# A GRU with a residual on one core: one block of GpSimd sums a step earlier, step 118 divided otherwise, nine units in front of the first state product

## The chip, the core and the metric

The kernel runs on one core of a Trainium2 chip. The metric is the device time of one execution in microseconds (us). TensorE (PE in the profile) multiplies matrices and writes into PSUM, VectorE (DVE) and ScalarE (ACT) read PSUM and SBUF, GpSimd (POOL) does elementwise work on SBUF, SyncE (SP) issues DMAs.

## The reference

x has 64 sequences of 128 steps with 512 features; h0 is 64 x 512. The output is x plus the states of a gated recurrent unit:

```python
z = sigmoid(concat([x_t, h]) @ Wz + bz)
r = sigmoid(concat([x_t, h]) @ Wr + br)
h_cand = tanh(concat([x_t, r * h]) @ Wh + bh)
h_new = (1.0 - z) * h + z * h_cand
h_next = where(prop, tanh(h_new @ Wp + bp), h_new)   # prop: every fourth step, not the last
# out[:, t] = x[:, t] + h_new
```

The products of h depend on the step before and must run one step behind the other; those of x do not.

## The kernel before

**The state products.** The batch of 64 is cut into two halves of 32, which are two Python generators, `half(0)` and `half(1)` (line 836). A loop at the end (line 947) runs whichever has issued less so far, so their instructions alternate in PE's queue. Each step does, per half: the R gate (`gate(R, ...)`, four products of h with 128 rows each), sigmoid on ACT, r*h and its turn (`rhT`, a transpose) on DVE; the Z gate; the H gate, which needs `rhT`; tanh on ACT; then on DVE the new h in three operations (L912, L921, the turn L251 into `hT`). In every fourth step the product with Wp follows. These products are the lines "rec<-wh" and "rec_z<-wh" of the profile.

**The x products as filler.** While PE would wait for ACT and DVE, it runs units of the x products from one list, `queue`. `fill(n, h)` (line 416) issues the next n units of a half. How many stand at which place of a step is written out by hand in `PLACES`, `HEAD` (line 626) and `TAIL` (line 627): three numbers per step, for the units behind the Z gate (line 903), behind the H gate (line 930) and behind the product with Wp (line 942). A step without an entry of its own uses `PLACES` by its place u in a period of eight; u = 3 has (6, 8, 0) and so has u = 2. Step 118 is `T - 10`, step 117 is u = 2. Before step 0, `both(n)` (line 632) runs the first n units for both halves, and step 0 has a fill of its own between the R and Z gates (line 863).

**The fast product.** For steps 2 and 3 the units are plain (`plain`, line 459): one unit is one block of 128 features and one gate. From group 1 (steps 4 to 7) on, the x products of groups of four steps are formed by a scheme of Strassen's kind on two levels: 7 outer blocks, each by 7 inner products, with sums of weights and of x formed beforehand and sums of results afterwards. `sum_inner(i)` (line 312) makes the sums of weights of outer block i: four operations, L318 to L321, of 128x384 elements. `sum_raw12`, `sum_raw4` and others make sums of x, each by `four` (line 325; L329 to L332), into buffers such as `s12r` and `s4r` that exist once. `batch` (line 483) makes the units of two blocks: 14 units, in an order fixed by their PSUM banks a, x or y, q and r. At certain units an `end` function runs behind the second half's unit: ACT copies a bank (L514), DVE adds it into `mb` (L531, L532, L537, L540, L541). `end_r2` (line 539; L540 and L541) is the last of a batch; L540 is the last reader of bank scratch_r, which the next batch writes again. The results are then summed on GpSimd (`pair_left`, `pair_right`, the `outer_` functions; L575 and L580 in the profile) into `cp`, and ACT seeds the gates' PSUM with that (L398).

**GpSimd's order.** Its instructions run in the order in which the generators write them. `behind_r` (line 724) is called by the second half behind the R gate, `behind_step` (line 757) at the end of a step. Around the change the order is: step 1 makes the sums of block 6, step 2 `pair_left(0, 1, 2)` in `behind_r`, then `sum_raw12(2)`, `sum_s12(2)` and the output's add (L811); step 3 `pair_right(0, 1, 10)` and `sum_inner(7)` in `behind_r`, then `pair_left(1, 8, 9)`, `pair_right(1, 8, 11)`, `sum_s34(2)`; step 4 `sum_inner(4)`; steps 5 and 6 the first sums of group 2, with `sum_raw4(2)` into `s4r`.

Of the kernel before, what the change touches and what calls it, by code (L numbers as in the profile page):

```python
# [18 lines left out]
def kernel(  # L19
# [14 lines left out]
    nc = tc.nc  # L34
    B, T, D = x.shape
# [7 lines left out]
    K = D // P  # L43
# [187 lines left out]
    def gate(i, h, lT, w):  # L231
        for k in range(K):
            products(gate_ps(i, h), h, lT[:, h, ts(k, V)], lambda c: quarters(w)[:, c, k])
            yield S * J
# [47 lines left out]
    def inner(i, ka, na):  # L282
        return OPERAND[i](ka)[:, :, :, ts(na, J // 4)]

    def leftover(i):
        return din[:, i - 1] if i <= 3 else inner(i, 0, 1)
# [25 lines left out]
    def sum_inner(i, eng, gates=slice(0, 3)):  # L312
        def of(v):
            return v[:, :, gates]

        t = [of(tt[:, i - 1, n]) for n in range(3)]
        v = {ab: of(inner(i, *ab)) for ab in ((0, 0), (0, 1), (1, 0), (1, 1))}
        eng.tensor_sub(t[1], v[1, 1], v[0, 1])  # L318
        eng.tensor_add(t[0], t[1], v[0, 0])
        eng.tensor_sub(t[2], v[1, 0], t[0])  # L320
        eng.tensor_sub(of(leftover(i)), v[0, 1], v[0, 0])  # L321
# [88 lines left out]
    def put(units):  # L410
        for unit, cols, bank, end, read in units:
            queue.append((unit, cols, reader.get(bank, -1), end))
            for b in read:
                reader[b] = len(queue) - 1

    def fill(n, h):
        for _ in range(n):
            if place[h] == len(queue):
                return
            unit, cols, after, end = queue[place[h]]  # L420
            while h == 0 and after >= place[1]:
                yield 0
            unit(h)
            yield cols
            place[h] += 1
            if h == 1 and end is not None:
                end()
# [31 lines left out]
    def plain(t, gates=(R, Z, H_)):  # L459
        order = [(e, k) for e in gates for k in range(K)]  # L460
        if t == Q4 - 1:
            order = [(e, k) for k in range(K) for e in gates]
        return [
            plain_unit(
                t,
                e,
                k,
                k == 0,
                *((lambda: add_bias(t, gates), gates) if t > 1 and (e, k) == order[-1] else ()),
            )  # L470
            for e, k in order
        ]
# [101 lines left out]
    def add(dst, a, b):  # L574
        nc.gpsimd.tensor_add(dst, a, b)  # L575

    def with_bias(g, i, v):
        m = M[g, i].rearrange("p b d g u -> p b (d g u)")
        v = v.rearrange("p d g u -> p (d g u)")
        nc.gpsimd.tensor_add(m, m, v.unsqueeze(1).to_broadcast([P, 2, 3 * J]))  # L580

    def c_block(g, a, nb):
        new_cp(2 * g + a)
        return flat(cp[2 * g + a][:, nb])

    def m_(g, i):
        return flat(M[g, i])
# [17 lines left out]
    def outer_u2(g):  # L605
        add(m_(g, 7), m_(g, 7), m_(g, 6))
# [7 lines left out]
    def pair_left(a, p1, p2, g=1):  # L614
        with_bias(g, p2, bias0)
        add(c_block(g, a, 0), m_(g, p1), m_(g, p2))

    def pair_right(a, p1, x_, g=1):
        with_bias(g, x_, bias_x[:, 1])
        add(c_block(g, a, 1), m_(g, p1), m_(g, x_))  # L620
# [4 lines left out]
    )  # L625
    HEAD = {0: (4, 6, 0), 1: (8, 6, 0), 2: (16, 12, 0), 3: (8, 6, 8), 4: (6, 8, 0)}
    TAIL = {
        T - 10: (5, 9, 0), T - 9: (1, 7, 5), T - 8: (1, 7, 0), T - 7: (1, 5, 0), T - 6: (0, 5, 0),
        T - 5: (0, 4, 3), T - 4: (0, 5, 0), T - 3: (0, 4, 0), T - 2: (0, 4, 0), T - 1: (0, 0, 0),
    }  # L630

    def both(n):
        for _ in range(n):
            for h in range(S):
                for _ in fill(1, h):
                    pass
# [42 lines left out]
    sum_outer(3)  # L679
    later_loads()  # L680
    put(plain(2, (R, Z)) + plain(3) + plain(2, (H_,)))
    both(6)

    state = {0: (h_init, hT)}

# [38 lines left out]
    def behind_r(t, duo, u):  # L724
        odd = FIRST + 2 * duo + 1
        if t == 2:
            pair_left(0, 1, 2)
        elif t == 3:
            pair_right(0, 1, 10)
            sum_inner(7, nc.gpsimd)  # L730
        if t == 4:
            sum_inner(4, nc.gpsimd)
        if u == 0 and duo >= 1 and odd - 2 < LAST:
            outer_u2(odd - 2)
# [101 lines left out]
    def half(h):  # L836

        for t in range(T):
# [10 lines left out]
            if h == 1:  # L849
                behind_r(t, duo, u)  # L850
# [9 lines left out]
                join(t, duo, u, 0)  # L860

            if t == 0:
                yield from fill(2 * K, h)
            yield from gate(Z, h, hT, wh[Z])
            keep = new_two("keep", t)
            z_ = z
# [79 lines left out]

    LAG = 700
    halves = [half(0), half(1)]
    at = [0, LAG]
    live = [True, True]  # L950
    while any(live):
        h = 0 if live[0] and (not live[1] or at[0] <= at[1]) else 1
# [46 lines left out]
```

## Time and profile before

| | us |
|---|---|
| median of 3 runs | 1262.54 (1262.44 to 1262.56) |
| the profiled execution | 1262.99 |
| its span, first to last instruction | 1261.0 |
| TensorE busy in it | 1250.6 |
| GpSimd busy in it | 891.3 |
| granted TensorE clock, mean | 0.999 |

A row of a timeline is: start and length in us, engine, line of the kernel, operation, what it writes and what it reads, partitions by elements, count; in brackets the idle time of the engine before it and what ended that. The rows of PE merge matmuls of one kind. A product of one unit is several records, and the two halves work side by side on different columns of the array.

### The profile page before, as it was taken

What the parts mean: (1) busy time and instruction counts of PE and PEld (TensorE: products, weight loads), DVE (VectorE), ACT (ScalarE), POOL (GpSimd) and SP (SyncE); (2) the same over time, 40 slices, a digit from 0 to 9 for tenths busy, and PEclk for the clock granted to TensorE, in tenths of its full rate; (3) what the DMA queues carried; (4) which work ended last, traced back from release to release, by engine and by line L of the source; (5) the groups of instructions that cost most, each with busy time, mean ns of one, the idle gap of its engine ahead of it and who ended that gap; (6) DMA issues with size and microseconds to landing.
All of it is one profiled execution on the core that took longest, in us unless ns stands there. A gap on an engine that the chain in (4) does not pass through costs nothing.

```text
span 1261.0 us, 60731 instructions
## 1 busy us (share of the span) xinstructions
PE 1250.6 (99%) x25960; PEld 1157.8 (92%) x25960; DVE 804.7 (64%) x2171; ACT 835.6 (66%) x2685; POOL 891.3 (71%) x1033
## 2 busy tenths in 40 slices
PE   9999999999999999999999999999999999999998
PEld 4898899999999999999999999999999999999875
DVE  4665666666666666666666666666666666666544
ACT  2566666666666766666676667666676766667665
POOL 3898867777776778767778677777777687677530
PEclk9999999999999999999999999999999999999999
DMA  8311111111121111221211111111111111111010
GB/s 238 92 27 44 46 45 51 38 50 40 37 53 44 45 45 28 53 53 37 53 28 44 53 43 47 39 47 40 53 36 53 40 33 53 48 42 36 7 43 24
DMA packets 113172, 60.82 MB, mean 48 GB/s; under 512 B 12776, under 2 KB 109288, under 8 KB 112904
## 3 DMA queue, kind: packets, MB, share of 16 engines
q1 hardware_dynamic: 111172, 54.97, 16.4%
q8 instruction: 205, 3.36, 1.1%
q10 hardware_dynamic: 1476, 1.84, 0.5%
q14 instruction: 63, 0.52, 0.1%
q0 software_dynamic: 256, 0.14, 0.1%
HBM read 40.11 MB, written 16.78 MB: 45 GB/s over the span
## 4 chain that ended last, share of the span: by engine, by line
PE 94%; POOL 2%; DMA 1%; SPq 1%; DVE 0%; issue 0%; ACT 0%; ACTq 0%; POOLq 0%; DVEq 0%
PE rec L222 43%; PE rec_z L222 16%; PE scratch_r L222 13%; PE scratch_q L222 10%; PE scratch_a L222 5%; PE scratch_x L222 4%; PE scratch_y L222 4%; POOL cp L575 1%; SPq L821 1%; POOL mb L580 1%; DMA wx<-in_L_cond_Wz_dram 1%; DMA xr<-in_x_dram 0%; DMA out_dram<-xr 0%; POOL xr L811 0%; POOL mb L575 0%
## 5 line engine op out<-in xcount | busy, mean ns | idle before, releaser
L222 PE MATMUL rec<-wh,rhT 128*32 128x256 f32 x4096 | 376.2, 379 | 0.0
L222 PE MATMUL rec<-wh,hT 128*32 128x256 f32 x3072 | 282.6, 379 | 0.4 <-DVE hT L251 0.4
L222 PE MATMUL rec_z<-wh,hT 128*32 128x256 f32 x3072 | 282.6, 379 | 0.0
L222 PEld LDWEIGHTS rec<-wh,rhT 128*32 128x32 f32 x4096 | 248.8, 110 | 20.1 <-ACT rec L398 0.9
L248 ACT ACTIVATE scratch_r<-rec 64x128 f32<-64x128 f32 x512 | 128.0, 250 | 137.7 <-PE rec L222 69.5
L398 ACT COPY rec<-cp 64x256 f32<-64x256 f32 x512 | 189.8, 371 | 20.6 <-DMA xr<-in_x_dram 1.1
L222 PEld LDWEIGHTS rec_z<-wh,hT 128*32 128x32 f32 x3072 | 192.2, 110 | 9.3
L222 PEld LDWEIGHTS rec<-wh,hT 128*32 128x32 f32 x3072 | 186.2, 110 | 14.6 <-ACT z L248 1.2
L248 ACT ACTIVATE rec_z<-rec_z 64x128 f32<-64x128 f32 x488 | 122.0, 250 | 91.8 <-PE rec_z L222 80.3
L248 ACT ACTIVATE c<-rec 64x128 f32<-64x128 f32 x512 | 138.9, 271 | 61.7 <-PE rec L222 50.1
L811 POOL TENSOR_TENSOR xr<-xr,h 128x256 f32<-128x256 f32 x127 | 93.0, 732 | 92.0 <-DVE h L921 89.3
L575 POOL TENSOR_TENSOR mb<-mb,mb 128x768 f32<-128x768 f32 x58 | 106.2, 1831 | 67.0 <-DVE mb L541 67.0
L575 POOL TENSOR_TENSOR cp<-mb,mb 128x768 f32<-128x768 f32 x76 | 139.0, 1829 | 8.1 <-DVE mb L541 4.4
L575 POOL TENSOR_TENSOR cp<-mb 128x768 f32<-128x768 f32 x46 | 84.2, 1831 | 56.8 <-ACT rec_z L398 55.4
L222 PE MATMUL scratch_r<-tw,s 128*32 128x192 f32 x928 | 120.8, 326 | 0.0
L514 ACT COPY cq<-scratch_q 128x384 f32<-128x384 f32 x212 | 102.1, 481 | 19.8 <-PE scratch_q L222 18.4
L531 DVE TENSOR_TENSOR cx<-scratch_r,cx 128x384 f32<-128x384 f32 x106 | 59.0, 557 | 84.8 <-PE scratch_r L222 67.5
L222 PE MATMUL scratch_q<-tt,s 128*32 128x192 f32 x928 | 103.6, 326 | 0.0
L873 DVE SCALAR_TENSOR_TENSOR keep<-rec_z,h 128x256 f32<-128x256 f32 x91 | 38.6, 424 | 95.8 <-ACT rec_z L248 88.5
L537 DVE TENSOR_TENSOR mb<-scratch_q,cx 128x384 f32<-128x384 f32 x106 | 59.1, 557 | 62.5 <-ACT cq L514 62.5
L853 DVE TENSOR_TENSOR rh<-scratch_r,h 128x128 f32<-128x128 f32 x192 | 56.0, 292 | 61.6 <-ACT scratch_r L248 61.6
L222 PE MATMUL rec<-wp,hT 128*32 128x256 f32 x992 | 91.5, 379 | 0.1
(188 smaller groups left out, 3840.0 us busy)
## 6 DMA issues: line engine op xcount, KB each, us to landing
out_dram<-xr SPq DMA_DIRECT2D x249, 64.0 KB, 1.8
xr<-in_x_dram SPq DMA_DIRECT2D x248, 64.0 KB, 2.0
xs<-in_x_dram SPq DMA_DIRECT2D x240, 64.0 KB, 2.0
wx<-in_L_cond_Wr_dram SPq DMA_DIRECT2D x2, 512.0 KB, 4.9
wx<-in_L_cond_Wz_dram SPq DMA_DIRECT2D x1, 1024.0 KB, 7.0
wx<-in_L_cond_Wh_dram SPq DMA_DIRECT2D x1, 1024.0 KB, 10.0
wp<-in_L_cond_Wp_dram SPq DMA_DIRECT2D x4, 256.0 KB, 5.7
wh<-in_L_cond_Wr_dram ACTq DMA_DIRECT2D x2, 256.0 KB, 4.7
```

Source lines behind the costliest of these rows:

```text
L222: nc.tensor.matmul(ps[part(2 * h + c)], lhsT=left, rhs=rhs(c), start=start, stop=True, skip_group_check=True,)
L248: nc.scalar.activation(dst[ts(d, 2 * V)], gate_ps(i, h)[ts(h, 2 * V), d, :], func)
L398: nc.scalar.copy(gate_ps(i, h)[rows].rearrange("p d (c n) -> p d c n", c=C), G[t][rows, :, :, i, :].rearrange("p c d n -> p d c n"),)
L514: nc.scalar.copy(c[:, :nm], ps[:, :nm])
L531: nc.vector.tensor_add(T2[what][:, :nm], r_ps[:, :nm], T2[what][:, :nm])
L537: nc.vector.tensor_add(blocks(1, 1), runs(q_ps[:, :nm]), runs(T2[what][:, :nm]))
L575: nc.gpsimd.tensor_add(dst, a, b)
L580: nc.gpsimd.tensor_add(m, m, v.unsqueeze(1).to_broadcast([P, 2, 3 * J]))
L811: nc.gpsimd.tensor_add(xr[g][:, j], xr[g][:, j], h_new)
L821: nc.sync.dma_start(out=out[ts(h, V), t - n + 1 : t + 1, ts(q, J)], in_=xr[g][part(q), j - n + 1 : j + 1, h, :],)
L853: nc.vector.tensor_mul(rh[:, h, :], r_, h_old[:, h, :])
L873: nc.vector.scalar_tensor_tensor(out=keep[:, part, :], in0=z_[:, part, :], scalar=1.0, in1=h_old[:, part, :], op0=ALU.subtract, op1=ALU.mult,)
```

## The change

Three places are edited. The four sums of the seventh inner block are written in step 2 instead of step 3. In step 118 six units of x stand behind the Z gate and eight behind the H gate, instead of five and nine. Nine units instead of six are issued in front of the first state product, and step 0's own fill has 5 units instead of 8 (K is 4). The instructions are the same in number and kind.

```diff
     TAIL = {
-        T - 10: (5, 9, 0), T - 9: (1, 7, 5), T - 8: (1, 7, 0), T - 7: (1, 5, 0), T - 6: (0, 5, 0),
+        T - 10: (6, 8, 0), T - 9: (1, 7, 5), T - 8: (1, 7, 0), T - 7: (1, 5, 0), T - 6: (0, 5, 0),
...
     put(plain(2, (R, Z)) + plain(3) + plain(2, (H_,)))
-    both(6)
+    both(9)
...
         if t == 2:
             pair_left(0, 1, 2)
+            sum_inner(7, nc.gpsimd)
         elif t == 3:
             pair_right(0, 1, 10)
-            sum_inner(7, nc.gpsimd)
...
             if t == 0:
-                yield from fill(2 * K, h)
+                yield from fill(2 * K - 3, h)
             yield from gate(Z, h, hT, wh[Z])
```

## The prediction

> **What bounds the kernel now.** The page comes first: its span and the busy time of each engine.
>
> ```profile
> span 1261.0 us, 60731 instructions
> PE 1250.6 (99%) x25960; PEld 1157.8 (92%) x25960; DVE 804.7 (64%) x2171; ACT 835.6 (66%) x2685; POOL 891.3 (71%) x1033
> ```
>
> TensorE (PE) computes for 1250.6 of 1261.0 us; no other engine passes 71%. No edit takes a matmul away, so the change can win only from the 10.4 us in which PE stands still, or lose by making PE stand still elsewhere. Second view: what PE waited for (total, times, longest).
>
> ```profile
> PE scratch_x L222 <- POOL s4r L331: 1.1, 1, 1.1
> PE scratch_r L222 <- DVE mb L540: 0.8, 1, 0.8
> ```
>
> The two longest each happen once, so each has a place; the others lie at the start, where the first loads are awaited, or are 0.2 us. The table by stretches finds it (length, then busy time of PE, PEld, DVE, ACT, POOL; clock, DMA).
>
> ```profile
> 20.00:25.00 5.00, 5.00 (x95) 3.03 (x91) 3.95 (x10) 0.20 (x1) 0.83 (x2) 1.00 1.05 254
> 100.00:105.00 5.00, 3.89 (x87) 3.32 (x82) 3.14 (x9) 2.45 (x8) 4.92 (x7) 1.00 0.14 37
> 1180.00:1190.00 10.00, 9.19 (x198) 7.62 (x191) 5.75 (x18) 6.13 (x21) 6.16 (x4) 1.00 0.01 2
> ```
>
> PE loses 1.11 us between 100 and 105 us, where GpSimd (POOL) is busy throughout, and 0.81 us between 1180 and 1190. From 20 to 25 us, where the third edit works, it loses nothing. The clock is 1.00 in all three.
>
> **First edit: the seventh inner block's sums.** Busy time counts the modelled tail of the matmul before a wait, so I price a stop by starts. The timeline of PE around it:
>
> ```profile
> 100.79 0.36 PE L222 MATMUL scratch_a<-wx,xT 128*32 128x192 f32 x2
> 100.83 0.39 PE L222 MATMUL rec<-wh,rhT 128*32 128x256 f32 x2
> 100.95 0.36 PE L222 MATMUL scratch_a<-wx,xT 128*32 128x192 f32 x2
> 102.42 0.36 PE L222 MATMUL scratch_x<-tt,s4r 128*32 128x192 f32 x2 [1.11 <-POOL s4r L331]
> 102.44 0.41 PE L222 MATMUL rec<-wh,rhT 128*32 128x256 f32 x2
> ```
>
> One half of the batch starts a pair every 0.16 us (100.79, 100.95); its next comes at 102.42: 1.47 - 0.16 = 1.31 us lost. The other half, which needs nothing from POOL, loses as much, since PE keeps its order: 102.44 - 100.83 = 1.61, less the 0.22 us at which its pairs of 256 columns follow each other (48 records, four at a time, in 2.59 us, in the rows of the third edit), 1.39. Mean 1.35 us. Now the POOL timeline that leads there:
>
> ```profile
> 54.24 1.83 POOL L575 TENSOR_TENSOR cp<-mb 128x768 f32<-128x768 f32 x1
> 60.49 0.46 POOL L329 TENSOR_TENSOR s12r<-xT 128x128 f32<-128x128 f32 x1 [4.42 <-PE scratch_r L222]
> 68.30 1.84 POOL L575 TENSOR_TENSOR cp<-mb,mb 128x768 f32<-128x768 f32 x1
> 70.09 1.01 POOL L318 TENSOR_TENSOR tt<-tw 128x384 f32<-128x384 f32 x1
> 74.20 1.85 POOL L580 TENSOR_TENSOR mb<-mb,bias_x 128x768 f32<-128x768 f32 x1
> 102.05 0.32 POOL L331 TENSOR_TENSOR s4r<-xT 128x64 f32<-128x64 f32 x1
> ```
>
> POOL idles 4.42 us before 60.49: the buffer s12r is free only when PE has read it. The four sums of block 7 run from 70.09 to 74.20. By starts they take 74.20 - 70.09 = 4.11 us. In step 2 they stand behind pair_left, whose last add (54.24) ends at 56.07, so they run until 56.03 + 4.11 = 60.14, 0.35 us before the next sum starts anyway. Their input tw[3] is POOL's own, written earlier in its queue, and nothing reads their results before the batches of group 2. Cost there: 0, covered by the idle time. The Trainium skill (Perfetto Trace Analysis, GPSIMD Engine Instruction) calls POOL's spans unreliable and starts the better clock; four spans of 1.01 as in the L318 row would give 4.04 and a spare of 0.42, and the same answer.
>
> What it frees is not 4.11 us. The instruction behind, pair_left for blocks 8 and 9, adds a bias to sums that DVE writes last here:
>
> ```profile
> 72.02 0.55 DVE L541 TENSOR_TENSOR mb<-scratch_x,cq 128x384 f32<-128x384 f32 x1
> 91.16 0.55 DVE L541 TENSOR_TENSOR mb<-scratch_x,cq 128x384 f32<-128x384 f32 x1
> 95.89 1.83 POOL L575 TENSOR_TENSOR mb<-mb,mb 128x768 f32<-128x768 f32 x1
> ```
>
> They are complete at 72.57, so POOL now waits from 70.1 to about 72.6 and starts 74.20 - 72.6 = 1.6 us earlier than before. From there to 102 it has no idle time, and I went through its inputs: the tightest is a block that DVE ends at 91.71 and POOL takes at 95.89, then at 94.3, still 2.6 us later. So the third sum of s4r ends at 102.37 - 1.6 = 100.8. PE wants it at 100.95 + 0.16 = 101.11, its weight load at 100.95. The wait goes, with 0.15 to 0.3 us to spare. **Worth 1.35 us**; bounds 0 (POOL held again) and 1.39. Behind 102 us both PE (1.35) and POOL (1.6) are earlier, so POOL's lead grows; the stores of step 3 and the loads behind them on SP's queue leave 1.6 us earlier, needed by nobody then.
>
> **Second edit: step 118.** The stop in PE's timeline, then DVE's timeline of step 118 and of step 117, which already runs with six and eight units:
>
> ```profile
> 1180.01 0.36 PE L222 MATMUL scratch_q<-wx,xT 128*32 128x192 f32 x2
> 1180.06 0.33 PE L222 MATMUL scratch_x<-tt,s4r 128*32 128x192 f32 x2
> 1181.20 0.36 PE L222 MATMUL scratch_r<-tw,s4r 128*32 128x192 f32 x2 [0.81 <-DVE mb L540]
> 1181.21 0.36 PE L222 MATMUL scratch_x<-tt,s12r 128*32 128x192 f32 x2
> ```
>
> ```profile
> 1167.98 0.56 DVE L537 TENSOR_TENSOR mb<-scratch_q,cx 128x384 f32<-128x384 f32 x1 [0.37 <-ACT cq L514]
> 1168.46 0.55 DVE L540 TENSOR_TENSOR mb<-scratch_r,cq 128x384 f32<-128x384 f32 x1
> 1177.82 0.56 DVE L537 TENSOR_TENSOR mb<-scratch_q,cx 128x384 f32<-128x384 f32 x1 [0.47 <-ACT cq L514]
> 1180.39 0.31 DVE L251 STREAM_TRANSPOSE hT<-h 128x128 f32<-128x128 f32 x1
> 1180.63 0.52 DVE L540 TENSOR_TENSOR mb<-scratch_r,cq 128x384 f32<-128x384 f32 x1
> ```
>
> Lost: 1181.20 - 1180.01 - 0.16 = 1.03 and 1181.21 - 1180.06 - 0.16 = 0.99, mean 1.01 us. Cause: with five units behind the Z gate, the batch's last unit comes behind the H gate, so DVE gets the read of its bank (L540) behind both turns of h (1180.39), and the next batch's first unit on scratch_r waits for it. In step 117 the sixth unit lies ahead of the H gate and L540 follows L537 at once; L537 of the two steps lies 9.84 us apart, so L540 will start near 1168.46 + 9.84 = 1178.30 and end at 1178.9, over 1 us before PE asks. Queued behind L540 and L541 on DVE are the state's own three operations, as in step 117, behind which the next state product starts at 1171.10:
>
> ```profile
> 1171.10 0.41 PE L222 MATMUL rec<-wh,hT 128*32 128x256 f32 x2
> ```
>
> No wait stands before it. Both steps do 14 units, so what follows keeps its place. **Worth 1.01 us**; bounds 0 and 1.03.
>
> **Third edit: nine units first.** Three units go from between the R and Z gates of step 0 to ahead of the R gate.
>
> ```profile
> 20.21 2.77 PE L222 MATMUL scratch_q<-wx,xT 128*32 128x256 f32 x48
> 22.80 1.50 PE L222 MATMUL rec<-wh,hT_init 128*32 128x256 f32 x20
> 21.66 0.65 DVE L264 STREAM_TRANSPOSE xT<-xr 128x256 f32<-128x256 f32 x1
> 27.05 0.31 DVE L251 STREAM_TRANSPOSE rhT<-rh 128x128 f32<-128x128 f32 x1
> 31.43 0.39 PE L222 MATMUL rec<-wh,rhT 128*32 128x256 f32 x2
> ```
>
> Six units take 22.80 - 20.21 = 2.59 us, so three take 1.30 and the R gate starts at 24.10. The ninth unit is the first on x of step 3; it starts at 20.21 + 8 x 0.43 = 23.67, and its transpose ends at 22.31: 1.36 us in hand. The last rhT moves from 27.36 to 28.66; the H gate keeps its place at 31.43, so the cover shrinks from 4.07 to 2.77 us and still holds. PE has no idle time to win here. **0**; bounds 0 and the 0.22 us of one pair.
>
> **The sum.** 1.35 + 1.01 + 0 = 2.36 us. The profiled execution took 1262.99 us (span 1261.0 and 2.0 outside it), 0.45 above the median of the runs, 1262.54. I carry the difference over: 1260.6 for a profile, **1260.2 us** for the runs. 0.2% of 1262.54, about what a measurement of this kernel can tell from no change, is 2.5 us: the forecast falls just inside.
>
> **The rivals.**
> *POOL is held again.* If anything between 72.6 and 100.8 holds POOL for d us, all but the spare 0.3 comes back as waiting for s4r. For it: the spare is small, and 4.92 of 5 us busy leaves no slack to catch up in. Against: every input that I followed is there. With half of the 1.35 gone: 1260.9; with all, 1261.5.
> *Step 118 only moves its wait.* L540 and L541 (0.9 us of DVE) now stand ahead of the state's operations; if step 119's first product then waited for hT, most of 1.01 would return: 1261.1. Against: step 117's rows.
> *Slower than before: the sums miss the gap.* If they can start only at 60.4, with the instruction that now ends the idle time, the chain behind shifts by 4.11 us. It leads to ACT and PE in step 3:
>
> ```profile
> 70.17 0.38 ACT L398 COPY rec_z<-cp 128x256 f32<-128x256 f32 x1 [0.43 <-POOL cp L575]
> 71.08 0.56 DVE L537 TENSOR_TENSOR mb<-scratch_q,cx 128x384 f32<-128x384 f32 x1 [0.75 <-ACT cq L514]
> 72.52 0.34 PE L222 MATMUL scratch_q<-wx,xT 128*32 128x192 f32 x2
> ```
>
> ACT already waits for POOL's add (68.30) there; behind that copy in its queue stands the one that DVE's L537 needs, and L537 is the last reader of scratch_q. It ends at 71.64, 0.88 us before PE writes the bank at 72.52. A shift of 4.11 stops PE for 3.2 us; the s4r wait then vanishes by itself (-1.35), step 118 gives -1.01: 1263.4. Shifts beyond 0.9 cost time; the kernel gets slower from 3.2. Against: all inputs of the sums stand earlier in POOL's own queue.
> *The sums fit, but run longer beside DVE.* The row of that stretch:
>
> ```profile
> 55.00:60.00 5.00, 5.00 (x122) 4.51 (x118) 2.80 (x8) 2.52 (x8) 1.07 (x1) 1.00 0.40 96
> ```
>
> If POOL stood still whenever DVE works, the sums would take up to 2.8 us longer, pass the gap by 2.45 and stop PE for 1.6: 1261.8. Against: between 70.09 and 74.20 three adds of DVE (71.08 to 72.57) run beside the same sums, and 4.11 contains that. The Trainium skill (SBUF — State Buffer, Who interferes with whom) has a DVE operation with two SBUF inputs and a reading GpSimd one lock each other out; DVE's adds here take one input from PSUM (rec_z, scratch), which by that section never locks.
>
> **How the numbers follow.** Forecast 0.69 (1259.8 to 1260.6, from the bounds, the pair and a tenth for the reading of starts); POOL held 0.15; step 118 0.08; slower 0.04; longer beside DVE 0.02; others 0.02. The range reaches to POOL's full loss and leaves the last three out: 1259.8 to 1261.5. Faster by over 0.2% means below 1260.0: a third of the forecast's case, 0.23. Slower by over 0.2% (above 1265.1) needs a shift of POOL by 5.8 us, or a cause that I don't see: 0.03. Same: 0.74.
>
> **What would show it.** Right: no idle time of POOL before 60.49, one of about 2.5 us before the L580 near 72.6, PE without a wait for s4r, 5.00 of 5 us from 100 to 105; in step 118 L540 directly behind L537 and no wait on it; PE unbroken from 20 to 40 with the R gate at 24.1. Wrong: a new wait of PE for POOL between 100 and 125, for hT near step 119, or for xT near 23.7.

## The result, and the profile after

The changed kernel took 1260.53 us (median of 11 runs, 1259.89 to 1262.01), the kernel before 1262.56 beside it (1262.34 to 1264.86): ratio 0.9976, interval 0.9968 to 0.9985, that is 3.0 us faster (1.9 to 4.0). The forecast was 1260.2 us, and "the same within 0.2%" as the likeliest class; the time came out 0.3 us from it, the ratio on the other side of that bound. The measures of the same 22 runs differ: the medians lie 2.0 us apart, the means 2.6 (ratios 0.9984 and 0.9980), and the interval holds them all. The profiled execution took 1260.17 us.

The page of the changed kernel, its span and engines:

```profile
span 1258.2 us, 60730 instructions
PE 1250.2 (99%) x25960; PEld 1164.0 (93%) x25960; DVE 805.0 (64%) x2171; ACT 836.3 (66%) x2685; POOL 892.7 (71%) x1033
```

The changed kernel's waits of PE (total, times, longest), the whole list:

```profile
PE rec L212 <- DVE zeros L67: 1.2, 1, 1.2
PE scratch_q L222 <- DMA wx<-in_L_cond_Wr_dram: 0.7, 2, 0.4
PE rec L222 <- ACT c L248: 0.2, 1, 0.2
PE rec L222 <- DVE hT L251: 0.2, 1, 0.2
```

Both waits that the edits aimed at (1.1 us for s4r, 0.8 us for L540) are gone, and no new one above 0.2 us has come; the 1.2 us for zeros lie at the very start, before as after. The stretches (same columns as in the prediction) say the same: 5.00 of 5 and 10.00 of 10 us where PE lost 1.11 and 0.81.

```profile
20.00:25.00 5.00, 5.00 (x96) 3.03 (x90) 4.04 (x9) 0.00 (x0) 1.41 (x3) 1.00 1.02 303
100.00:105.00 5.00, 5.00 (x115) 4.73 (x111) 3.46 (x11) 3.59 (x11) 4.92 (x6) 1.00 0.07 17
1180.00:1190.00 10.00, 10.00 (x217) 9.33 (x212) 6.10 (x17) 6.76 (x23) 4.09 (x4) 1.00 0.02 4
```

POOL's timeline of the changed kernel around the moved sums, and where they came from:

```profile
53.63 1.83 POOL L575 TENSOR_TENSOR cp<-mb 128x768 f32<-128x768 f32 x1
55.41 1.01 POOL L318 TENSOR_TENSOR tt<-tw 128x384 f32<-128x384 f32 x1
...
58.54 1.01 POOL L321 TENSOR_TENSOR tw<-tw 128x384 f32<-128x384 f32 x1
59.84 0.46 POOL L329 TENSOR_TENSOR s12r<-xT 128x128 f32<-128x128 f32 x1 [0.29 <-PE scratch_r L222]
...
71.98 1.83 POOL L580 TENSOR_TENSOR mb<-mb,bias_x 128x768 f32<-128x768 f32 x1 [2.51 <-DVE mb L541]
...
99.83 0.32 POOL L331 TENSOR_TENSOR s4r<-xT 128x64 f32<-128x64 f32 x1
```

The sums fill the old gap of 4.42 us and leave 0.29 of it; behind, POOL waits 2.51 us for L541. DVE's timeline of step 118:

```profile
1175.70 0.56 DVE L537 TENSOR_TENSOR mb<-scratch_q,cx 128x384 f32<-128x384 f32 x1 [0.37 <-ACT cq L514]
1176.18 0.55 DVE L540 TENSOR_TENSOR mb<-scratch_r,cq 128x384 f32<-128x384 f32 x1
1176.64 0.55 DVE L541 TENSOR_TENSOR mb<-scratch_y,cq 128x384 f32<-128x384 f32 x1
...
1178.71 0.31 DVE L251 STREAM_TRANSPOSE hT<-h 128x128 f32<-128x128 f32 x1
```

L540 stands behind L537, ahead of both turns of h. Last, the third edit and the start, in PE's timelines. Of the kernel before, the first product that needs the Z part of wx:

```profile
11.45 1.93 PE L222 MATMUL scratch_q<-wx,xT 128*32 128x256 f32 x32 [0.37 <-DMA wx<-in_L_cond_Wz_dram]
```

Of the changed kernel, the same product and the first state product:

```profile
10.82 1.91 PE L222 MATMUL scratch_q<-wx,xT 128*32 128x256 f32 x32
...
23.44 1.93 PE L222 MATMUL rec<-wh,hT_init 128*32 128x256 f32 x28
```

The span splits at the first state product. In front of it: 22.80 us before, 23.44 after; that is 1.3 more for three units, and 0.65 less because the Z part of wx had landed in time (11.45 - 10.82 = 0.63). Behind it: 1261.0 - 22.80 = 1238.2 before, 1258.2 - 23.44 = 1234.8 after, 3.4 less: the three units that moved (1.3) and 2.1 of the 2.36 us forecast for the two stops. So of 2.8 us between the two profiles, 0.6 lie in front of every edited instruction.

### The profile page after: what moved, and what is told of

It reads as the page before. It is cut to its first block, busy times and chain, and to the rows that moved or that the text cites. A ratio compares the mean times of both kernels' runs of the same rounds, so it can differ in the third digit from the quotient of the medians.

```text
span 1258.2 us, 60730 instructions
## 1 busy us (share of the span) xinstructions
PE 1250.2 (99%) x25960; PEld 1164.0 (93%) x25960; DVE 805.0 (64%) x2171; ACT 836.3 (66%) x2685; POOL 892.7 (71%) x1033
## 4 chain that ended last, share of the span: by engine, by line
PE 98%; DMA 1%; ACT 0%; DVE 0%; issue 0%; DVEq 0%; ACTq 0%
PE rec L222 45%; PE rec_z L222 16%; PE scratch_r L222 14%; PE scratch_q L222 11%; PE scratch_a L222 5%; PE scratch_x L222 4%; PE scratch_y L222 4%; DMA wx<-in_L_cond_Wr_dram 0%; ACT z L248 0%; ACT c L248 0%; DMA xr<-in_x_dram 0%; DVE z L912 0%; PE scratch_x L194 0%; PE scratch_y L194 0%; DVE xr L915 0%
## 5 line engine op out<-in xcount | busy, mean ns | idle before, releaser
L537 DVE TENSOR_TENSOR mb<-scratch_q,cx 128x384 f32<-128x384 f32 x106 | 59.1, 558 | 62.4 <-ACT cq L514 62.4
```

Of the source, the lines that this page charges most:

```text
L537: nc.vector.tensor_add(blocks(1, 1), runs(q_ps[:, :nm]), runs(T2[what][:, :nm]))
```

## The experiments

Theory: edits 1 and 2 take away the two stops as priced; the scatter of the first loads moves single executions; edit 3 is worth something only in an execution where wh[R] (the R weights of the state) lands after PE is ready. Rival: edit 3 is worth nothing, and what exceeds 2.36 us is scatter of the start alone. Every kernel is timed beside runs of the kernel before; a ratio carries its 95% interval.

**One edit at a time.** Each of the three edits alone, in the form that the change has it.

> Only the first edit: the four sums of block 7 in step 2. Theory (the two waits are the whole gain): PE's wait for s4r is gone, the wait for L540 in step 118 and the start are as before, so 1.35 us less, a ratio near 0.9989. Rival (the third edit brings something too): the same here, 1.35 us; this run alone does not tell them apart, its sum with the next two does.

> Only the second edit: six and eight units in step 118. Theory: the wait for L540 is gone, the wait for s4r stays at 1.1 us, so 1.01 us less, a ratio near 0.9992. Rival (step 118 only moves its wait): a new wait for hT ahead of step 119 and no gain.

> Only the third edit: nine units ahead of the first state product. Theory: both long waits of PE stay, PE stays unbroken from 20 to 40 us, time unchanged within 0.2 us, ratio 1.0000. Rival (the edit covers a late landing of the weights of h in some executions, which a single trace need not show): 0.5 to 0.7 us less on average, ratio near 0.9995, and fewer slow outliers than the kernel before.

The fourth is edits 1 and 2 without the third, against the changed kernel:

```diff
-    both(9)
+    both(6)
...
-                yield from fill(2 * K - 3, h)
+                yield from fill(2 * K, h)
```

> The first and second edits without the third. Theory: both long waits are gone, 2.36 us less, ratio near 0.9981, as with all three. Rival (the third edit brings 0.6 us): 0.6 us above the kernel with all three.

| kernel | median us (before 1263.21) | ratio | first state product at | span behind it |
|---|---|---|---|---|
| edit 1 | 1261.62 | 0.9985 (0.9977 to 0.9994) | 22.62 | 1237.0 |
| edit 2 | 1262.23 | 0.9996 (0.9987 to 1.0005) | 22.50 | 1237.4 |
| edit 3 | 1262.99 | 1.0001 (0.9992 to 1.0010) | 24.23 | 1237.0 |
| edits 1 and 2 | 1261.41 | 0.9988 (0.9979 to 0.9997) | 24.71 | 1236.5 |

Of PE's waits with edit 1 alone:

```profile
PE scratch_r L222 <- DVE mb L540: 0.8, 1, 0.8
PE rec L222 <- DMA wh<-in_L_cond_Wr_dram: 0.4, 1, 0.4
```

With edit 2 alone:

```profile
PE scratch_x L222 <- POOL s4r L331: 1.1, 1, 1.1
```

With edit 3 alone:

```profile
PE scratch_x L222 <- POOL s4r L331: 1.1, 1, 1.1
PE scratch_r L222 <- DVE mb L540: 0.8, 1, 0.8
```

Each of the first two edits takes its own wait and leaves the other. The intervals are too wide to tell the two sizes from each other, and edit 2's contains 1.0000; the span behind the first state product, which the loads awaited ahead of it don't reach, fell from 1238.2 by 1.2 and 0.8. Edit 3 alone changed nothing that the time can show; the 1.2 us by which its part behind is shorter are its own three units, which now stand in front (24.23). New is the wait for wh[R] with edit 1 alone. It stands in PE's timeline with edits 1 and 2, too:

```profile
24.71 1.96 PE L222 MATMUL rec<-wh,hT_init 128*32 128x256 f32 x28 [0.37 <-DMA wh<-in_L_cond_Wr_dram]
```

Neither edit 1 nor 2 touches that load: two of these three profiles with six units in front show the wait, the kernel before does not. (The 1236.5 hold 0.6 more than the 1235.9 of the same kernel below: there the weight load of the Z gate stood 0.6 us for nothing that the profile names; the last piece of wh[Z] was issued at 19.1 us and took 11.0, so it landed at about 30.1, where that gate's first product starts, at 30.21.) That put edit 3's price of 0 in doubt. The kernel before was near it: its last piece of wh[R] was issued at 16.4 us and took 5.6, so it landed at 22.0, 0.8 us ahead of the first state product at 22.80.

**The whole change again, and once more without edit 3.** The changed kernel, and edits 1 and 2 alone.

> The changed kernel once more, timed beside its own shared runs of the kernel before. Theory (two waits removed, 2.41 us in the traces, and nine units that are worth something only in executions where the R weights land late): 2.4 to 2.9 us faster, ratio 0.9977 to 0.9981; in the profile no wait for s4r, none for mb at L540, none for wh. Rival (the first -3.0 us held 0.6 us of scatter of the start and nothing else): 2.4 us, ratio 0.9981, and no nearer to 0.9976 than the run without edit 3 of this call.

> Edits 1 and 2 without edit 3, once more. Theory (late R weights cost some executions 0.55 us when only six units stand in front): 0.2 to 0.6 us slower than the whole change in this call; a wait of PE for wh in the profile if the last piece of wh[R] lands after about 22.5 to 24.7 us (where PE stands ready), none if it lands sooner. Rival (scatter alone): equal to the whole change within 0.2 us.

Before took 1262.89 us. The whole change: 1260.90, 0.9981 (0.9972 to 0.9989), so 2.4 us faster. Without edit 3: 1260.85, 0.9987 (0.9978 to 0.9996). In both profiles wh[R] landed in time. The first state product in PE's timeline of the whole change (span 1258.5):

```profile
23.85 1.93 PE L222 MATMUL rec<-wh,hT_init 128*32 128x256 f32 x28
```

And without edit 3 (span 1258.2):

```profile
22.26 1.93 PE L222 MATMUL rec<-wh,hT_init 128*32 128x256 f32 x28
```

No wait stands before either. Behind the first state product are 1234.7 and 1235.9 us, 1.2 to 1.3 apart: the three units, and nothing else. The medians are equal here, which speaks for the rival; the ratios, 0.9976 and 0.9981 with edit 3 against 0.9988 and 0.9987 without, lean to the theory by about 1.1 us, with an uncertainty as large as that; the means of these two sets of 11 runs lie 0.4 us apart. Times alone don't settle a cost that only some executions have, so the next two kernels let wh[R] land late.

**Late weights.** The loads of wh[Z] are issued ahead of those of wh[R], with six and with nine units.

```diff
-    load_wh(R)
+    load_wh(Z)
     now(first[Z][1])
...
-    load_wh(Z)
+    load_wh(R)
```

> Edits 1 and 2, six units in front, and the loads of wh[Z] issued ahead of those of wh[R], so that wh[R] lands where wh[Z] landed so far (last piece at 25.7 to 27.3 us in the profiles) with PE ready at about 22.7. Theory: PE waits 2.9 to 4.5 us for wh at the first product of the state, and the time is 1261.0 + 3 to 4 = about 1264.5 us (slower than the kernel before by 1 to 2 us).

> The whole change with the same order of loads, so nine units in front of the late wh[R]. Theory (three units more are 3 x 0.43 us of work that fills such a wait): the wait is 1.29 us shorter than with six units for the same landing, and the time about 1.2 us lower, near 1263.2 us. Rival (the units have no worth here because PE is full and what is done earlier is missed later): the wait is shorter, but the time of both kernels is the same within 0.4 us, with a new idle time of PE behind, at the Z gate or before the turn of the state.

Six units: 1267.72 us (6 runs), 1.0036 (1.0024 to 1.0048). Nine: 1265.17, 1.0015 (1.0006 to 1.0024). Both are slower than expected (about 1264.5 and 1263.2). PE's timeline with six units (span 1264.2):

```profile
26.52 3.26 PE L222 MATMUL rec<-wh,hT_init 128*32 128x256 f32 x28 [3.94 <-DMA wh<-in_L_cond_Wr_dram]
```

With nine (span 1262.1):

```profile
27.41 1.96 PE L222 MATMUL rec<-wh,hT_init 128*32 128x256 f32 x28 [2.63 <-DMA wh<-in_L_cond_Wr_dram]
```

The stretch of 3 us behind the wait, six units (the granted clock is the third number from the end):

```profile
26.50:29.50 3.00, 2.98 (x29) 1.80 (x31) 0.00 (x0) 0.00 (x0) 2.92 (x4) 0.58 1.12 204
```

And nine:

```profile
27.40:30.40 3.00, 2.99 (x52) 2.24 (x54) 0.38 (x2) 0.88 (x4) 2.92 (x4) 1.00 1.09 215
```

The wait is 1.31 us shorter with three more units, as expected, and no new wait appears behind. The ratios are 0.0021 apart, 2.7 us, twice the expected 1.2. In these two executions the stretches show a second cost: after 3.94 us of standing still the granted clock is 0.58 in the next stretch, and the same 28 records take 3.26 us; after 2.63 us it is 1.00, and they take 1.96. The Trainium skill (TensorE: Matmul & The Clock Gate, What's actually happening) has the clock halved after an idle window of about 3.4 us; the trace agrees. In the other runs only the mean clock is on record: it is 0.997 or 0.998 in five of the six runs with six units, and 0.996 to 0.998 in seven of the eleven with nine, where most runs with the usual order of loads have 0.999 or 1.000. So both medians hold some cost of the clock, and how much of the 2.7 us it makes up is not shown.

**A little late.** Half of wh[Z] ahead of wh[R], for a wait short enough to leave the clock alone.

```diff
+    load_wh(Z, (0, 2))
     load_wh(R)
...
-    load_wh(Z)
+    load_wh(Z, (1, 3))
```

> Edits 1 and 2, six units in front, and half of wh[Z] (two of its four loads) issued ahead of wh[R], so that the last piece of wh[R] lands about 2.5 us later than in the kernel before (near 23.5 to 24.5 us, with PE ready near 22.5). Theory: PE waits 0.8 to 2 us for wh, under the 2.6 us that cost no clock in the run with nine units and late weights; the time is higher by that wait than without the late half: 1261.9 to 1263 us. Rival (a wait there is given back later, where POOL would have been late anyway): a wait in the profile, but 1261.0 to 1261.4 us.

> The whole change with the same half of wh[Z] issued ahead of wh[R]. Theory: three units cover 1.29 us of the wait, so 0 to 0.7 us of it are left and the time is 0.8 to 1.3 us below that with six units: 1260.9 to 1261.8 us. Rival (given back later): the same time as with six units within 0.3 us.

Before took 1263.55 us; six units 1264.36, 1.0009 (0.9997 to 1.0021); nine 1263.49, 1.0008 (0.9998 to 1.0017). The medians differ by 0.9 us, the ratios by nothing, and the runs of each lie 4 to 6 us apart: inconclusive as times, and both slower than expected, since this order of loads landed later than I worked out (with six units PE waited 2.85 us, not 0.8 to 2). Nor did the clock stay out of it in every run: five of the eleven with six units and three of the twelve with nine show a mean of 0.996 to 0.998. In the two profiled ones it was 0.999 and 1.000. PE's timeline with six units (span 1261.5):

```profile
25.49 1.96 PE L222 MATMUL rec<-wh,hT_init 128*32 128x256 f32 x28 [2.85 <-DMA wh<-in_L_cond_Wr_dram]
```

With nine (span 1261.7; "issue" is a wait whose releaser the profile doesn't show, and the view ends before the last of the 28 records):

```profile
27.05 1.31 PE L222 MATMUL rec<-wh,hT_init 128*32 128x256 f32 x16 [2.27 <-issue]
```

PE waited in both, with six units for wh[R]; that it was wh[R] with nine units too is inferred from the place. So the landing set when the first state product started, 25.49 and 27.05; behind it stand 1236.0 and 1234.7 us, as in the runs with the weights in time (1235.9 and 1234.7). So nothing is given back: an execution takes the later of "PE ready" and "landed", plus 1236.0 with six units or 1234.7 with nine, as long as the clock stays at 1.00 and the Z weights are in time. Where PE is ready first by w, edit 3 is worth w, up to 1.3 us; where the weights are there, 0. This shows its mechanism. How often w is above 0 in the usual order of loads, these runs don't settle: a mean clock below 0.999, as behind the long stops, stands in 4 of 160 runs with six units (1264.83 to 1269.74 us) and in none of 44 with nine, too few to tell, and what stopped PE in them is not on record.

**The same work without the wait.** Six units, and step 0's R gate takes its weights from wx, so that gate is computed from other numbers.

```diff
-            yield from gate(R, h, hT, wh[R])
+            yield from gate(R, h, hT, wh[R] if t else wx[:, :, R, :])
```

> Edits 1 and 2 with six units in front, and the R gate of step 0 takes its weights from wx in place of wh (so step 0's R gate is computed from other numbers; as many products, and no wait for the R weights of the state). Theory (edit 3 is worth something only where wh[R] lands late): no wait for wh in the profile at the first state product, and runs like those of the whole change: median 1260.3 to 1260.9 us, highest below 1262.5 us. Rival (edit 3 gains in another way than by that wait): as without edit 3, mean about 1261.4 to 1261.6 us and single runs above 1263 us.

Before took 1263.28 us; this one 1261.13 (1260.03 to 1262.68), 0.9981 (0.9972 to 0.9990): the ratio of the second measurement of the whole change. Yet the median and the highest run each lie 0.2 us above the theory's bounds (1260.9 and 1262.5), and the mean, 1261.3, lies just below the rival's 1261.4 to 1261.6, though no run lies above 1263 as the rival had it: the times do not decide between the two. The profile shows another limit. The start of POOL's long chain in this kernel's timeline:

```profile
26.25 0.17 POOL L676 COPY held<-d 1x1 f32<-1x1 f32 x1 [5.84 <-DVE d L310]
```

The same in the changed kernel:

```profile
23.52 0.17 POOL L676 COPY held<-d 1x1 f32<-1x1 f32 x1 [5.83 <-DVE d L310]
```

Two of PE's waits in this kernel:

```profile
PE scratch_x L222 <- POOL s4r L331: 0.4, 1, 0.4
...
PE scratch_q L222 <- DVE mb L537: 0.2, 1, 0.2
```

Here POOL starts 2.9 us behind the first state product (23.36), in the changed kernel 0.1; 1.3 of the difference are the three units, so POOL is 1.5 us late against PE. With that the wait for s4r is back, 0.4 us, and PE waits 0.2 for the reader of scratch_q that the slower rival named: in this execution it is POOL's lead that runs out behind the start.

**The sums miss the gap.** The kernel before with the sums behind the s12r sums of step 2: the prediction's slower rival, made real.

```diff
+        if t == 2:
+            sum_inner(7, nc.gpsimd)
...
         elif t == 3:
             pair_right(0, 1, 10)
-            sum_inner(7, nc.gpsimd)
```

> The kernel before with one move: the four sums of the seventh inner block stand in step 2 behind the s12r sums, so POOL's 4.42 us of idle time before 60.49 us is not used and all that follows on POOL is about 4.1 us later. Theory (the slower rival of the prediction): the wait for s4r is gone (-1.35 us), and PE stops for about 3.2 us at its first scratch_q product near 72.5 us, behind the late addition at L580: +1.9 us, about 1264.4 to 1264.8 us, ratio near 1.0015. Rival (only the place behind step 3 matters, PE doesn't feel a POOL that is 4 us late): no stop there, about 1.35 us faster than the kernel before, ratio 0.999, like edit 1.

1266.32 us, 1.0029 (1.0018 to 1.0040): slower, and above the 1264.4 to 1264.8 expected. Of PE's waits:

```profile
PE scratch_q L222 <- DVE mb L537: 3.0, 1, 3.0
...
PE rec_z L222 <- DMA wh<-in_L_cond_Wz_dram: 0.4, 1, 0.4
PE scratch_x L222 <- POOL s4r L331: 0.4, 1, 0.4
```

PE's timeline at the stop:

```profile
72.50 0.36 PE L222 MATMUL scratch_y<-tt,s12r 128*32 128x192 f32 x2
72.54 0.33 PE L222 MATMUL scratch_a<-wx,xT 128*32 128x192 f32 x2
75.90 0.36 PE L222 MATMUL scratch_q<-wx,xT 128*32 128x192 f32 x2 [3.03 <-DVE mb L537]
75.92 0.36 PE L222 MATMUL scratch_a<-wx,xT 128*32 128x192 f32 x2
```

POOL's timeline, the start of the chain and its place behind that stop:

```profile
60.65 0.46 POOL L329 TENSOR_TENSOR s12r<-xT 128x128 f32<-128x128 f32 x1 [4.81 <-PE scratch_r L222]
...
76.86 1.83 POOL L580 TENSOR_TENSOR mb<-mb,bias_x 128x768 f32<-128x768 f32 x1 [2.51 <-DVE mb L541]
```

The stop comes at the place and, priced by starts as in the prediction (75.90 - 72.50 - 0.16 = 3.24, 75.92 - 72.54 - 0.16 = 3.22), at the size that the rival had (3.2). But the wait for s4r shrinks from 1.1 to 0.4 only, where "the s4r wait then vanishes by itself" stood. POOL's L580 waits for L541, which the same stop delays: it starts at 76.86, 2.66 us later than the 74.20 before, so PE, some 3 us later, gains only some 0.4 to 0.7 us on it. 3.2 less 0.7, and 0.4 more in this execution for the Z weights of the state, make 2.9; the part behind the first state product (at 22.39 us, span 1263.7) is 1241.3 us against 1238.2, 3.1 more. The profiled execution is the fastest of the nine, with a mean clock of 0.999; seven of the others show 0.996 to 0.998, so the median may hold a cost of the clock as well.

**More of the same.** The changed kernel with 14 units in front, and one with a unit moved from step 120 to step 121.

```diff
-    both(9)
+    both(14)
...
-                yield from fill(2 * K - 3, h)
+                yield from fill(2 * K - 8, h)
```

> The whole change with 14 units, not nine, in front of the first state product (8 units less behind step 0's R gate). Theory: nothing more to gain once wh[R] is covered, 0 to 0.3 us against the whole change (wh[Z], whose last piece lands at 25.3 to 30.1 us, is no later covered than before, since the Z gate stays where it was), and the turn of step 0's rh is still hidden: about 1260.5 to 1260.9 us. Rival (every unit in front gains, 0.2 us each three): 0.4 us less. A third: with 8 units left behind the R gate, PE waits for rhT, and the time is over 1261.5 us.

```diff
-T - 8: (1, 7, 0), T - 7: (1, 5, 0)
+T - 8: (1, 6, 0), T - 7: (1, 6, 0)
```

> The whole change, and one unit of x moved from step 120 to step 121 (divisions (1,6,0) and (1,6,0) for (1,7,0) and (1,5,0)). In the trace of the changed kernel PE loses about 1.1 us from 1204.7 to 1209.4 us, behind the turns of step 121; a unit is 0.43 us for both halves. Theory: 0.2 to 0.4 us faster than the whole change. Rival: the loss moves to the turns of step 120, and the time is the same within 0.2 us.

Fourteen units: 1261.39 us, 0.9979 (0.9970 to 0.9987). One unit in the tail: 1261.24, 0.9983 (0.9975 to 0.9992). Against 0.9976 and 0.9981 for the whole change neither can be told from it: no version is shown to beat it, and gains of 0.2 to 0.4 us, which the expectations had, are too small for these intervals. Fourteen units brought no wait for rhT.

## Why the prediction was right, and where it was wrong

**What bounds the kernel** held for edits 1 and 2: each gain was a stop of PE with one place and one releaser. The start is different: there the loads, and after a long stop the clock, move single executions.

**First edit** (1.35 us): right in its steps; with edit 1 alone the part behind the first state product fell by 1.2. The changed execution runs 0.65 us early from its start. Taking that out, POOL starts L580 at 71.98 + 0.65 = 72.63 ("about 72.6", waiting 2.51, "about 2.5"), and the third sum of s4r ends at 99.83 + 0.32 + 0.65 = 100.80 (100.8). The gap left before s12r is 0.29, forecast 0.35.

**Second edit** (1.01 us): right in its steps; with edit 2 alone that part fell by 0.8. L540 was put at 1178.30; with 0.65 and 1.35 taken off that is 1176.30, and it started at 1176.18. No wait for hT took its place.

**Third edit** (0): the first of two steps that failed. "PE has no idle time to win here" was read from one execution, in which wh[R] had landed 0.8 us before PE came to it. I followed what the three units need (x, its transpose) and what they cover (rhT), but not the DMA that the product behind them waits for, and how near its landing stood to PE. The term is not 0 with a bound of 0.22, but the wait for wh[R] up to 1.3 us: 0.4 in two of six profiles with six units and the usual order of loads, 0 in four. That is 0.13 us on average, and edit 3 alone measured 1.0001 (0.9992 to 1.0010), so a larger average worth is not shown.

**The sum and its class.** "Same", with 0.74, is the second step that failed. It took 0.2%, 2.5 us, for what a measurement of this kernel can tell from no change; the intervals measured here reach about 1.1 us to each side, so that a gain of 2.36 us is told from none, as both measurements of the whole change did. And the forecast lay less than 0.2 us inside that bound: with a third term that can only gain, and with a start whose loads alone move the first state product, faster and same should have had about equal chances. The two measurements, 3.0 and 2.4 us, fall on either side of the bound. By the part behind the first state product edits 1 and 2 are worth 2.1 to 2.3 us (1238.2 to 1235.9 with six units; 3.4 less the 1.3 of the moved units with nine), so they do not carry the first one's 0.6 us above the sum; how much of it is edit 3 and how much the scatter of the start stays open. That the median came within 0.3 us of the forecast is in part luck, since the start alone moves single executions by more than that.

**The rivals.** POOL held again and step 118 moving its wait did not come. The slower rival's mechanism is real at the price it was given for the stop (3.2 us); its sum was too low, because the stop that PE suffers delays POOL as well. The sums longer beside DVE: 59.55 - 55.41 = 4.14 us from the first start to the last end, beside 4.11 before from the first start to the next instruction's.

## What to carry to other kernels

An engine that is busy without a gap in one trace can still stand before a load that landed just in time: for each product that is the first to need a DMA, compare the landing with the moment at which the engine is ready, and work that can be put in front is worth the difference, in the executions that have it. Where a kernel's start waits for loads, split the span at the first product behind them: with nine units the part behind repeated to 0.1 us here, while the two medians of the whole change lay 0.4 apart. And when a stop is added, don't count another wait as gone before you have asked whether the same stop delays its releaser too.

## What the runs showed of the hardware

The clock: in the profiled execution with a stop of 3.94 us the granted clock was 0.58 in the 3 us behind it and 0.88 in the next 3.5, and the part from the first state product on was 1237.7 us, 1.8 more than the 1235.9 of the same units without a stop. Behind the stops of 2.63, 2.85 and 3.03 us that were profiled the clock was 1.00. That is one execution each; other runs of the same kernels had lower mean clocks, and their stops were not seen. The start: with the same loads in the same order, and PE ready or not, the first state product with six units came at 22.26 to 24.71 us in six profiles, so single executions differ by 2.5 us before the tuned part begins; against that, the two edits that show in every profile are worth 2.1 to 2.3.
